# Layer 4 of a graph network on one core: four open node tiles at the start, counts widened four pieces ahead, x and own parts loaded two tiles ahead

## The chip, the cores and the metric

The kernel runs on one core of one Trainium2 chip. The metric is the time of one execution on the device in microseconds (us). The kernel before took 2745.0 us (median of 3 runs, 2740.99 to 2750.39).

## The reference

Four GraphSAGE layers over 6250 nodes and 100,000 edges sorted by target node. Layer 4 and what follows it are the part that matters here:

```python
h = jnp.maximum(_layernorm(x, axis=-1), 0.0)
...                                                   # layers 1 to 3
msum = jax.ops.segment_sum(h[src], dst, num_segments=n)
h_neigh = msum / jnp.clip(deg, 1.0)[:, None]
h = h @ W4_self + h_neigh @ W4_neigh + b4
return x + (h @ W_fc + b_fc)
```

The kernel multiplies the weights together ahead of time. So a node of layer 4 needs three things: its input row of x, an "own part" of 256 values that layer 3 left in the table `xq`, and the sum, divided by the degree, of the rows of its source nodes. Those rows stand in the table `tab_s` with 512 float32 values each (a value of 256 features, split into two addends).

## The kernel before

The 6250 nodes are 49 tiles of 128 (`NT`). Many edges end in low nodes, so layer 4 sums in two ways that run side by side.

- **Hub tiles** 0 to 21 (`H4` = 22) are dense products (`dense`, the matmul at L566). A matrix of edge counts between 128 targets and 128 sources (fp8, from `tab_a`) is multiplied with the 128x512 rows of that source tile. A hub tile takes 49 such matmuls, added up in one PSUM bank `pd`. The counts come in pieces of 5 to 7 source tiles: `load` (L1785) fetches a piece `ac` on ScalarE's DMA queue, nine pieces ahead, and `widened` (L1794) has ScalarE cast it to a 32-bit `af`. A piece is cast two pieces ahead of its products, into one of four buffers. Eight pieces make a hub tile.
- **Sum tiles** 22 to 48 go over 266 groups of 128 edges (`sums`). For each, GpSimd starts an indirect DMA (L492) that gathers 128 rows of `tab_s` into one of 14 slots of `ring`. VectorE makes a one-hot matrix `hot` (L488), TensorE multiplies (L510, into `pg`), and VectorE adds four such groups' result to the tile's `acc` (L542, L544). `hub.advance` mixes the hub matmuls in between, about four to one gather.

The source rows are kept in SBUF as eight resident tiles `zt`. Two of them, source tiles 33 to 42, are filled by layer 3. The other six are fetched from `tab_s` by SyncE (L1817) when layer 3 has ended: zt0, zt7, zt14, zt20, zt27 and zt43, named by their first source tile. Before, hub tiles 0 and 1 are opened first: their 20 products on the two kept `zt` run ahead of the gathers, then both are finished in turn, then tiles 2 to 21 follow.

When a tile is summed, `done4` calls `load4`: ScalarE's queue fetches the tile's x (`xr`, L1893) and own part (`q`, L1895), 10 buffers each. `finish4` adds the two on VectorE (L1909), adds the scaled sum (L1911), and SyncE stores the tile (L1914). For sum tiles the next tile's two loads are issued as well.

The program is written in the order of this text, but a scheduler places each engine's instructions by its own estimate of when operands and buffers come free. After that each engine runs its queue strictly in order; a DMA that has to wait holds up all that stands behind it in its queue. The plain (not gathered) DMAs of the ScalarE and SyncE queues also take turns on eight semaphores (DMAHW0 to DMAHW7). A DMA that gets a semaphore first waits until that semaphore's last user has landed, whatever queue and data that was.

Of the kernel before, what the change touches and what calls it, by code (L numbers as in the profile page):

```python
# [13 lines left out]
F32R = mybir.dt.float32r  # L14
# [7 lines left out]
P = 128  # L22
# [15 lines left out]
def _edges_below(n, E, N):  # L38

    f = math.sqrt(min(n, N) / N)  # L40
    return E * f, Z_SIGMA * math.sqrt(E * f * (1.0 - f))
# [37 lines left out]
def fast_path(  # L79
# [19 lines left out]
    FO = W_fc.shape[1]  # L99
    NT = (N + P - 1) // P  # L100
# [15 lines left out]
    for d in range(NT):  # L116
        m, s = _edges_below(d * P, E, N)
        m1, s1 = _edges_below((d + 1) * P, E, N)
# [9 lines left out]
    for d in range(NT):  # L128
        m, s = _edges_below(d * P, E, N)
        m1, s1 = _edges_below((d + 1) * P, E, N)  # L130
# [7 lines left out]
    H1, H3, H4 = HUB  # L138
# [112 lines left out]
    one_tag = {}  # L251
# [304 lines left out]
    def dense(ss, block, rows, F, psd, done, extra=0, wide=False, own=None, halved=()):  # L556

        hold = {}

        def run(s):  # L560
            if s == ss[0]:
                hold[0] = bank(psd, "pd", "pd", (2 * F if wide else F + extra,))
            a = block(s)
            z = rows(s)
            if wide:
                nc.tensor.matmul(hold[0], a, z, start=(s == ss[0]), stop=(s == ss[-1]))  # L566
            order = () if wide else (1, 0) if s in halved else (2, 0, 1)
            for part in order:
                c = extra if part == 2 else 0
                first = s == ss[0] and part == order[0]  # L570
                if s == own:
                    nc.tensor.matmul(hold[0], ident_r if s in halved else ident_b,
                                     z[:, part * F : (part + 1) * F], start=first, stop=False)
                nc.tensor.matmul(hold[0][:, : F + c], a, z[:, part * F : (part + 1) * F + c],  # L574
                                 start=(first and s != own),
                                 stop=(s == ss[-1] and part == order[-1]))
            if s == ss[-1]:
                done(hold[0])

        return [lambda s=s: run(s) for s in ss]  # L580
# [4 lines left out]
    ahead = upto2.enter_context(tc.tile_pool(name="ahead", bufs=1, side="right"))  # L585
# [77 lines left out]
    with ExitStack() as pro:  # L663
        pst = pro.enter_context(tc.tile_pool(name="pst0", bufs=3, space=PSUM))
        psm = pro.enter_context(tc.tile_pool(name="psm0", bufs=3, space=PSUM))
# [193 lines left out]
        nk = max(RB1, RB * P - RB1)  # L859
# [239 lines left out]
    with ExitStack() as on:  # L1099
        pst = on.enter_context(tc.tile_pool(name="pst1", bufs=1, space=PSUM))  # L1100
        psm = on.enter_context(tc.tile_pool(name="psm1", bufs=1, space=PSUM))
        psg = on.enter_context(tc.tile_pool(name="psg1", bufs=2, space=PSUM))
        psd = on.enter_context(tc.tile_pool(name="psd1", bufs=2, space=PSUM))
        wk = on.enter_context(tc.tile_pool(name="fl1", bufs=2))
# [30 lines left out]
        def done1(d, acc):  # L1135
# [37 lines left out]
            with behind(ended):  # L1173
                for k in range(KI):
# [11 lines left out]
                        lambda acc, d=d: todo.append(done1(d, acc)), extra=3)  # L1186
# [4 lines left out]
        hub = Hub(made.rest() + work)  # L1191
# [124 lines left out]
    with tc.tile_pool(name="fl2c", bufs=1) as ck, ExitStack() as late:  # L1316
        pst = psm = late.enter_context(tc.tile_pool(name="pst2", bufs=3, space=PSUM))
        one_tag[id(pst)] = "pw"
        psd = late.enter_context(tc.tile_pool(name="psd2", bufs=2, space=PSUM))
# [58 lines left out]
        wk = late.enter_context(tc.tile_pool(name="fl2", bufs=2))  # L1378
# [242 lines left out]
        def widened(got):  # L1621
            if 1 not in got:
                got[1] = early_pool[0].tile([P, BATCH, P], F32R, name="aw", bufs=4)
                nc.scalar.copy(got[1], got[0])  # L1624
# [36 lines left out]
        for _ in range(7):  # L1661
# [3 lines left out]
        first = [w for d in range(H1, H4)  # L1665
                 for w in build_narrow(d, (skR, mkR, RB1), npool, psb, copies)]
        hub = Hub(first, 12)
# [12 lines left out]
        for b in reversed(range(NB)):  # L1680
# [3 lines left out]
            for s0 in range(0, tb, G2):  # L1684
                X = (xmore if at // G2 % 2 else xpool).tile([P, G2, FH], F32, name="X2")
                for k in range(G2):
# [27 lines left out]
                    if at == MADE_AT:  # L1714
                        for _ in steps:
# [3 lines left out]
                                                    name="kept_rows", bufs=1))  # L1719
# [51 lines left out]

    upto2.close()

    def stream(pool, chunks, wide_pool=None, widen=lambda s: True, deep=4):

        got = {}
        where = {(d, s): i for i, (d, s0, s1) in enumerate(chunks) for s in range(s0, s1)}

        def load(i):
            if i >= len(chunks):  # L1780
                return
            d, s0, s1 = chunks[i]
            got[i] = pool.tile([P, 7, P], F8, name="ac", bufs=deep + 1)
            t = got[i][:, : s1 - s0, :]
            nc.scalar.dma_start(t.bitcast(BF16), tab_a[d, :, s0:s1, :])  # L1785

        wide = {}
        most_wide = max([s1 - s0 for _, s0, s1 in chunks if widen(s0)])

        def widened(i):  # L1790
            if i < len(chunks) and widen(chunks[i][1]):
                n = chunks[i][2] - chunks[i][1]
                wide[i] = wide_pool.tile([P, most_wide, P], F32R, name="af", bufs=4)
                nc.scalar.copy(wide[i][:, :n, :], got[i][:, :n, :])  # L1794

        for i in range(deep):
            load(i)
        if wide_pool:
            widened(0)
            widened(1)  # L1800

        def block(d, s):
            i = where[d, s]
            if s == chunks[i][1]:
                if wide_pool:
                    widened(i + 2)
                load(i + deep)
            return (wide if i in wide else got)[i][:, s - chunks[i][1], :]

        return block  # L1810
# [10 lines left out]
    with ExitStack() as on:  # L1821
        psd = on.enter_context(tc.tile_pool(name="psd3", bufs=2, space=PSUM))
        psg = on.enter_context(tc.tile_pool(name="psg3", bufs=3, space=PSUM))
        psm = on.enter_context(tc.tile_pool(name="psm3", bufs=2, space=PSUM))
        zk = on.enter_context(tc.tile_pool(name="fz4", bufs=1, side="right"))
        Z4 = {}
        z4_kept = ((33, 38), (38, 43))
        z4_late = ((0, 7), (7, 14), (14, 20), (20, 27), (27, 33), (43, NT))
# [4 lines left out]
        with tc.tile_pool(name="fl3", bufs=2) as wk:  # L1833
# [37 lines left out]
            with tc.issue_after(kept_stores[-1].ins):  # L1871
                for s0, s1 in ((EARLY[1], NT),):
                    Z3.update(resident(wk, tab_r, FH, s0, s1))
            block = stream(wk, [(d, s0, s1) for d in range(H3) for s0, s1 in late], wk,
                           lambda s: s < KEPT)
            todo = []
            work = []
            for d in range(H3):
                work += dense([s for s0, s1 in late for s in range(s0, s1)], lambda s, d=d: block(d, s), lambda s: Z3[s], FH, psd,
                              lambda acc, d=d: todo.append(done3(d, acc)), own=d,  # L1880
# [6 lines left out]
        with tc.tile_pool(name="fl4", bufs=2) as wk:  # L1887
            loaded4 = {}

            def load4(d):  # L1890
                n = P if d < NFULL else NREM
                xr = wk.tile([P, FI], F32, name="xr4", bufs=10)
                nc.scalar.dma_start(xr[:n, :], x[d * P : d * P + n, :])  # L1893
                q = wk.tile([P, FO], F32, name="q4", bufs=10)
                nc.scalar.dma_start(q[:n, :], xq[d * P : d * P + n, :])  # L1895
                loaded4[d] = n, xr, q

            def done4(d, acc):
                for i in (d, d + 1) if H4 <= d < NT - 1 else (d,):
                    if i not in loaded4:  # L1900
                        load4(i)
                return finish4(d, acc)

            def finish4(d, acc):
                n, xr, q = loaded4.pop(d)
                yield 1
                yield 1
                yield 1
                nc.vector.tensor_add(xr[:n, :], xr[:n, :], q[:n, :])  # L1909
                for c in range(0, acc.shape[1], FO):  # L1910
                    nc.vector.scalar_tensor_tensor(xr[:n, :], acc[:n, c : c + FO],  # L1911
                                                   rmean[:n, d : d + 1], xr[:n, :],
                                                   op0=ALU.mult, op1=ALU.add)
                nc.sync.dma_start(out[d * P : d * P + n, :], xr[:n, :])  # L1914

            order = [*z4_kept, *z4_late]
            block = stream(zk, [(d, *c) for d in (0, 1) for c in z4_kept]
                           + [(d, *c) for d in (0, 1) for c in z4_late]
                           + [(d, *c) for d in range(2, H4) for c in order],
                           wk, deep=9)  # L1920
            todo = []
            parts4 = []
            for d in range(H4):
                parts4.append(dense([s for s0, s1 in order for s in range(s0, s1)],
                                    lambda s, d=d: block(d, s), lambda s: Z4[s], FO, psd,
                                    lambda acc, d=d: todo.append(done4(d, acc)), wide=True))
            nk = sum(s1 - s0 for s0, s1 in z4_kept)
            hub = Hub([w for d in (0, 1) for w in parts4[d][:nk]]
                      + [w for d in (0, 1) for w in parts4[d][nk:]]
                      + [w for p in parts4[2:] for w in p])  # L1930
            hub.advance(2 * nk)
            for s0, s1 in z4_late:
                Z4.update(resident(wk, tab_s, FO, s0, s1))
            sums(wk, psg, tab_s, FO, srcE, keyE, jb, H4, done4, 14, hub, wait=4, todo=todo,
                 rest=8, wide=True)

# [642 lines left out]
```

## Time and profile before

| | |
|---|---|
| median of 3 runs | 2745.0 us |
| the profiled execution's own time | 2742.18 us |
| its span in the trace | 2740.4 us |
| granted TensorE clock, mean | 0.922 |
| first matmul of layer 4 | 2357.81 us |
| last matmul | ends 2728.45 us |
| busy shares over the span | PE 84%, DVE 76%, POOL 68%, ACT 47% |

The time outside the span is 2742.18 - 2740.4 = 1.8 us. Layer 4 is the last 383 us of the span and is the only part that the diff touches. PE is TensorE, PEld its weight loads, DVE VectorE, ACT ScalarE, POOL GpSimd, SP SyncE; a q behind the name is the engine's sequencer, which issues its DMAs. "idle before" names what an engine was waiting for when it stood still.

### The profile page before, as it was taken

To read this page: it belongs to the slowest core of one execution; us is meant where nothing else is said; L and a number is where in the kernel's file an instruction comes from. 1 tells how busy PE (TensorE), PEld (TensorE's weight loads), DVE (VectorE), ACT (ScalarE), POOL (GpSimd) and SP (SyncE) were. 2 spreads that over 40 slices of the span, in tenths; PEclk is the share of its full clock that TensorE was granted. 3 is DMA by queue.
4 is the path that set the end of the run, shared out by engine and by line. 5 is a ranking of instruction groups with operands and counts; after the bars stand their busy time and mean duration, and the time that the engine had idled before them with its cause. 6 is when DMAs were issued, how large, how long until landed. Compare 5 with 4: busy or idle time off the path is not lost.

```text
span 2740.4 us, 37738 instructions
## 1 busy us (share of the span) xinstructions
PE 2314.7 (84%) x10402; PEld 1439.0 (53%) x10402; DVE 2088.1 (76%) x5540; ACT 1299.7 (47%) x2859; POOL 1857.0 (68%) x2169
## 2 busy tenths in 40 slices
PE   4689999999786466566889999899799999789988
PEld 2356666767453232223555666655345444467776
DVE  8889777776589898898678998888376777446666
ACT  5568777764288888686423333232111111134443
POOL 5477777777566676677656676676477777657765
PEclk8799999999898588787999999999899999899999
DMA  8467777777799899899999999898899999999987
GB/s 279 152 179 209 209 208 213 217 232 221 222 356 333 299 346 336 283 336 361 328 290 301 339 349 322 275 341 292 300 376 387 381 380 351 347 323 316 319 286 226
DMA packets 365625, 809.90 MB, mean 296 GB/s; under 512 B 56238, under 2 KB 154646, under 8 KB 365372
## 3 DMA queue, kind: packets, MB, share of 16 engines
q0 software_dynamic: 143248, 501.86, 56.3%
q1 hardware_dynamic: 145928, 215.57, 21.6%
q10 hardware_dynamic: 76228, 89.96, 9.8%
q8 instruction: 85, 1.39, 0.2%
q14 instruction: 136, 1.11, 0.1%
HBM read 602.51 MB, written 205.46 MB: 295 GB/s over the span
## 4 chain that ended last, share of the span: by engine, by line
PE 48%; DMA 24%; DVE 13%; ACT 5%; issue 4%; POOL 2%; ACTq 0%; DVEq 0%; SPq 0%; POOLq 0%
PE pd L574 17%; PE pg L513 11%; DMA X<-rows,srcIf 7%; DMA xr<-in_x 4%; DVE run L1669 4%; DMA ring<-tab_h,srcT 4%; PE pm_hp L1175 3%; DMA rows<-X 3%; PE pm_prf L1558 3%; PE pm_hp L1169 2%; PE pd L566 2%; PE pb L349 2%; DVE acc L544 2%; DVE X L1669 2%; PE pm_prf L1552 2%
## 5 line engine op out<-in xcount | busy, mean ns | idle before, releaser
L1688 POOL DMA_INDIRECT X<-rows,srcIf x782 | 742.1, 949 | 368.9 <-issue 150.6
L1669 DVE SCALAR_TENSOR_TENSOR run<-run,samef,X 128x512 f32<-128x512 f32 x758 | 572.4, 755 | 49.0 <-DMA X<-rows,srcIf 43.5
L492 POOL DMA_INDIRECT ring<-tab_h,srcT x474 | 455.4, 961 | 149.9 <-issue 53.1
L513 PE MATMUL pg<-ring,hot 128*128 128x259 bf16 (+1 forms) x2292 | 475.1, 316 | 41.9 <-DMA ring<-tab_h,srcT 29.1
L544 DVE SCALAR_TENSOR_TENSOR acc<-pg,M,acc 128x256 f32<-128x256 f32 (+2 forms) x617 | 314.3, 536 | 80.9 <-PE pg L513 69.1
L492 POOL DMA_INDIRECT ring<-tab_r,srcE x290 | 293.3, 1011 | 116.2 <-issue 48.5
L1794 ACT CAST af<-ac 128x768 fp32r<-128x768 fp8e4 (+3 forms) x216 | 173.2, 805 | 398.9 <-DMA ac<-tab_a 157.8
L492 POOL DMA_INDIRECT ring<-tab_s,srcE x266 | 254.6, 957 | 124.6 <-PE pg L510 47.8
L566 PE MATMUL pd<-zt,af 128*128 128x512 f32 x1078 | 302.9, 407 | 38.1 <-ACT af L1794 31.6
L513 PEld LDWEIGHTS <-hot 128*128 128x128 bf16 x2292 | 214.3, 98 | 226.4 <-issue 103.6
L1669 DVE SCALAR_TENSOR_TENSOR X<-X,samef,run 128x512 f32<-128x512 f32 x379 | 282.1, 744 | 37.4 <-DMA X<-rows,srcIf 16.5
L574 PE MATMUL pd<-kept_rows,aw 128*128 128x512 f32 x920 | 292.2, 440 | 11.2 <-ACT aw L1624 6.3
L566 PEld LDWEIGHTS pd<-zt,af 128*128 128x128 f32 x1078 | 208.7, 196 | 95.8 <-ACT af L1794 44.6
L574 PEld LDWEIGHTS pd<-kept_rows,aw 128*128 128x128 f32 x920 | 174.7, 192 | 83.9 <-issue 35.3
L488 DVE TENSOR_SCALAR hot<-iota_bf,keyE 128x128 bf16<-128x128 bf16 (+1 forms) x556 | 142.9, 281 | 86.7 <-PE pg L513 55.3
L1558 PE MATMUL pm_prf<-unf,hTf 128*128 128x512 f32 x384 | 201.0, 647 | 1.9 <-ACT hTf L1548 1.3
L341 ACT ACTIVATE hs<-ht,onef 128x128 bf16<-128x128 bf16 x396 | 153.3, 393 | 89.4 <-PE pb L349 88.4
L1624 ACT CAST aw<-ae 128x512 fp32r<-128x512 fp8e4 x160 | 99.4, 622 | 181.3 <-PE pd L574 163.9
L574 PE MATMUL pd<-Z,A 128*128 128x256 bf16 (+1 forms) x1176 | 184.8, 274 | 0.7 <-ACT A L354 0.6
L375 ACT ACTIVATE ht<-iota_bf,skR 128x128 bf16<-128x128 bf16 x448 | 158.1, 402 | 11.0 <-DMA col<-in_L_gnn_b 8.0
L393 PE MATMUL pb<-hm,hs 128*128 128x196 bf16 x448 | 82.3, 281 | 89.8 <-ACT A L398 65.4
L340 ACT ACTIVATE ht<-iota_bf,sk 128x128 bf16<-128x128 bf16 x396 | 153.1, 398 | 8.3
(391 smaller groups left out, 4198.6 us busy)
## 6 DMA issues: line engine op xcount, KB each, us to landing
rows<-X SPq DMA_DIRECT2D x385, 256.0 KB, 4.9
tab_r<-r ACTq DMA_DIRECT2D x48, 384.0 KB, 5.9
rows<-hpf SPq DMA_DIRECT2D x49, 256.0 KB, 3.4
th<-tab_t ACTq DMA_DIRECT2D x49, 256.0 KB, 6.6
X<-rows,srcIf POOLq DMA_INDIRECT x782
tab_a<-A ACTq DMA_DIRECT2D x14, 784.0 KB, 6.0
ae<-tab_a SPq DMA_DIRECT2D x160, 64.0 KB, 5.0
tab_s<-q SPq DMA_DIRECT2D x39, 256.0 KB, 6.1
```

The source lines that it names most:

```text
L340: nc.scalar.activation(t, iota_b, AF.Abs, bias=sk[:, r : r + 1])
L341: nc.scalar.activation(hots[0], t, AF.Relu, bias=one, scale=-1.0)
L375: nc.scalar.activation(held["ht"][:, i, :], iota_b, AF.Abs, bias=sk[:, r : r + 1])
L492: nc.gpsimd.indirect_dma_start(out=ring[:, j % deep, :].bitcast(F32) if wide else ring[:, j % deep, :], out_offset=None, in_=table, in_off ...
L513: mm = nc.tensor.matmul(pg[:, : F + c], hot[j], X[:, part * F : (part + 1) * F + c], start=(k == 0 and part == 2), stop=(k == n - 1 and pa ...
L544: nc.vector.scalar_tensor_tensor(acc[d], half, m, acc[d], op0=ALU.mult, op1=ALU.add)
L566: nc.tensor.matmul(hold[0], a, z, start=(s == ss[0]), stop=(s == ss[-1]))
L574: nc.tensor.matmul(hold[0][:, : F + c], a, z[:, part * F : (part + 1) * F + c], start=(first and s != own), stop=(s == ss[-1] and part == ...
L1558: nc.tensor.matmul(pm, hT[:, c, :], un[:, c, :], start=False, stop=(c == KH - 1))
L1669: nc.vector.scalar_tensor_tensor(put, held, st, row, op0=ALU.mult, op1=ALU.max)
L1688: nc.gpsimd.indirect_dma_start(out=X[:, k, :], out_offset=None, in_=tab_p, in_offset=bass.IndirectOffsetOnAxis(ap=srcI[:, t : t + 1], axis=0),
L1794: nc.scalar.copy(wide[i][:, :n, :], got[i][:, :n, :])
```

## The change

Five edits, all in layer 4:

1. `widened` casts four pieces ahead of the products, and `af` has six buffers.
2. Hub tiles 0 to 3 are open together. Their products go piece by piece: the four tiles' first pieces, the four tiles' second pieces, and so on, through all eight. The 40 products on the two kept `zt` run ahead of the first gather's product.
3. The PSUM banks of hub tiles alternate between two pools in pairs, so that four can be open.
4. `done4` loads x and own part for the tile and the next two, for hub tiles too.
5. The stream of pieces is listed in the new order.

```diff
-    def stream(pool, chunks, wide_pool=None, widen=lambda s: True, deep=4):
+    def stream(pool, chunks, wide_pool=None, widen=lambda s: True, deep=4, ahead=2):
...
-                wide[i] = wide_pool.tile([P, most_wide, P], F32R, name="af", bufs=4)
+                wide[i] = wide_pool.tile([P, most_wide, P], F32R, name="af", bufs=ahead + 2)
...
-            widened(0)
-            widened(1)
+            for i in range(ahead):
+                widened(i)
...
-                    widened(i + 2)
+                    widened(i + ahead)
...
+        one_tag[id(psm)] = "pm"
...
-                for i in (d, d + 1) if H4 <= d < NT - 1 else (d,):
+                for i in range(d, min(d + 3, H4 if d < H4 else NT)):
...
-            block = stream(zk, [(d, *c) for d in (0, 1) for c in z4_kept]
-                           + [(d, *c) for d in (0, 1) for c in z4_late]
-                           + [(d, *c) for d in range(2, H4) for c in order],
-                           wk, deep=9)
+            first = range(4)
+            block = stream(zk, [(d, *c) for c in order for d in first]
+                           + [(d, *c) for d in range(4, H4) for c in order],
+                           wk, deep=9, ahead=4)
...
-                                    lambda s, d=d: block(d, s), lambda s: Z4[s], FO, psd,
+                                    lambda s, d=d: block(d, s), lambda s: Z4[s], FO, (psd, psm)[d // 2 % 2],
...
-            hub = Hub([w for d in (0, 1) for w in parts4[d][:nk]]
-                      + [w for d in (0, 1) for w in parts4[d][nk:]]
-                      + [w for p in parts4[2:] for w in p])
-            hub.advance(2 * nk)
+            cuts = [sum(s1 - s0 for s0, s1 in order[:i]) for i in range(len(order) + 1)]
+            hub = Hub([w for a, b in zip(cuts, cuts[1:]) for d in first for w in parts4[d][a:b]]
+                      + [w for p in parts4[4:] for w in p])
+            hub.advance(4 * nk)
```

TensorE, from the start of layer 4, before. zt_21030 and zt_21031 are the kept source rows, zt_24758, zt_24760 and zt_24762 are zt0, zt7 and zt14; `pg` are products of gathered rows:

```order
L566 MATMUL pd<-zt_21030,af 128x512 x5
L566 MATMUL pd<-zt_21031,af 128x512 x5
L510 MATMUL pg<-ring,hot 128x512 x5
L566 MATMUL pd<-zt_24758,af 128x512 x5
L510 MATMUL pg<-ring,hot 128x512
L566 MATMUL pd<-zt_24758,af 128x512 x2
L510 MATMUL pg<-ring,hot 128x512 x7
L566 MATMUL pd<-zt_24760,af 128x512 x7
L510 MATMUL pg<-ring,hot 128x512 x6
L566 MATMUL pd<-zt_24762,af 128x512 x6
```

(The first two rows stand there twice, once for each of the two tiles.) The same place in the changed program, where zt_24800 is zt0:

```order
L566 MATMUL pd<-zt_21030,af 128x512 x20
L566 MATMUL pd<-zt_21031,af 128x512 x20
L510 MATMUL pg<-ring,hot 128x512 x5
L566 MATMUL pd<-zt_24800,af 128x512 x5
L510 MATMUL pg<-ring,hot 128x512
L566 MATMUL pd<-zt_24800,af 128x512 x4
L510 MATMUL pg<-ring,hot 128x512
L566 MATMUL pd<-zt_24800,af 128x512 x4
```

Twice as many products run ahead of the first gather's product, and each late `zt` now serves 24 or 28 products, with one gather's product after every four or so, before the next `zt` is needed. Before, it served 6 or 7.

SyncE's queue, the loads of the late `zt` before, with the semaphores that each waits for:

```order
L1817 DMA zt7_24760<-tab_s_68 128x7x512
L1817 DMA zt14_24762<-tab_s_68 128x6x512 [waits DMAHW2_49]
L1817 DMA zt20_24764<-tab_s_68 128x7x512 [waits DMAHW3_49]
L1817 DMA zt27_24766<-tab_s_68 128x6x512 [waits DMAHW5_49]
L1817 DMA zt43_24768<-tab_s_68 128x6x512 [waits DMAHW4_49]
```

and in the changed program:

```order
L1817 DMA zt7_24802<-tab_s_68 128x7x512
L1817 DMA zt14_24804<-tab_s_68 128x6x512 [waits DMAHW6_49]
L1817 DMA zt20_24806<-tab_s_68 128x7x512 [waits DMAHW3_49]
L1817 DMA zt27_24808<-tab_s_68 128x6x512 [waits DMAHW3_49]
L1817 DMA zt43_24810<-tab_s_68 128x6x512 [waits DMAHW2_49]
```

The four last waits moved to other semaphores. By the values waited for, zt14 now waits for zt0 to land, zt20 for a piece of counts, zt27 for zt20, and zt43 for a piece of counts. Before, zt14, zt20, zt27 and zt43 waited for pieces of counts and own parts on ScalarE's queue.

ScalarE's queue in the changed program, at the casts of the four pieces for zt20 (af_25002 is the first tile's, the two casts above it are the last for zt14):

```order
L1794 CAST af_24962<-ac_24867 128x768 [waits PE_49]
L1896 DMA q4_25127<-xq_70 128x256 [waits DMAHW6_49]
L1785 DMA ac_25059<-tab_a_69 128x384 [waits DMAHW7_49,Activation_49]
L1894 DMA xr4_25129<-in_x 128x256 [waits DMAHW0_49]
L1794 CAST af_24977<-ac_24886 128x768 [waits PE_49]
L1896 DMA q4_25131<-xq_70 128x256 [waits DMAHW1_49]
L1785 DMA ac_25073<-tab_a_69 128x384 [waits DMAHW3_49,Activation_49]
L1794 CAST af_25002<-ac_24908 128x896 [waits PE_49]
```

Here the load of ac_25073 has the semaphore DMAHW3 after zt27, so it waits for zt27 to land, and the casts for zt20 stand behind it. In the same way the first cast for zt27 stands behind a load that waits for zt43. Before, the loads that wait for zt0, zt7, zt14 and zt20 stood on this queue, with eight loads of x and seven of own parts among them. In the changed program the first load of x stands behind the cast of the second piece for zt14.

## The prediction

> **What bounds the kernel now.** The diff touches layer 4 alone, so the table by stages comes first. Its columns are the stage, its length, the busy time of PE, PEld, DVE, ACT and POOL with instruction counts, the granted clock, the DMA engines' busy share and GB/s.
>
> ```profile
> 2357.80:2420.00 62.20, 41.37 (x98) 27.95 (x99) 19.01 (x62) 11.53 (x14) 38.83 (x41) 0.68 1.02 391
> 2420.00:2442.00 22.00, 22.00 (x98) 18.07 (x97) 11.57 (x34) 11.79 (x14) 8.88 (x10) 1.00 0.81 248
> 2442.00:2452.00 10.00, 10.00 (x46) 8.26 (x45) 7.28 (x23) 4.07 (x5) 7.56 (x9) 1.00 0.96 323
> 2452.00:2697.00 245.00, 227.43 (x964) 179.86 (x963) 155.79 (x485) 106.00 (x125) 179.12 (x187) 0.99 0.93 306
> 2697.00:2728.50 31.50, 31.50 (x140) 25.90 (x139) 21.85 (x68) 14.30 (x17) 20.24 (x21) 1.00 0.80 251
> ```
>
> PE's counts are matmuls of 512 columns, so they measure progress: 1344 are to be done (1078 hub, 266 gathered). Unhindered, one takes 31.5/140 = 0.225 us. In the first 62 us, the ramp, only 98 are done, the work of 22 us: 40 us are lost there. In the 245 us after 2452 one takes 0.254 us, and 28 us are lost. These are the two places where the change can win.
>
> The ramp waits for the late `zt`. The chain of waits has this in it (start, us, what):
>
> ```profile
> 2357.48 23.77 DMA zt<-tab_s
> 2381.33 0.33 ACTq L1785
> ```
>
> zt7 lands at 2381.25. A load of counts waited for that semaphore on ScalarE's queue, and the casts waited behind it. The timeline shows the next `zt` in the same way:
>
> ```profile
> 2357.81 7.58 PE L566 MATMUL pd<-zt,af 128*128 128x512 f32 x20 [5.64 <-ACT af L1794]
> 2371.12 2.34 PE L566 MATMUL pd<-zt,af 128*128 128x512 f32 x5
> 2392.64 2.90 PE L566 MATMUL pd<-zt,af 128*128 128x512 f32 x6 [4.99 <-DMA zt<-tab_s]
> 2406.30 0.33 ACTq L1785 DMA_DIRECT2D ac<-tab_a  x1
> 2406.70 0.36 SPq L1817 DMA_DIRECT2D zt<-tab_s  x1
> 2418.99 4.62 PE L566 MATMUL pd<-zt,af 128*128 128x512 f32 x19 [2.35 <-ACT af L1794]
> ```
>
> zt0 is there by 2371.1, zt14 at 2392.6, and the count load at 2406.3 is the one that waits for zt20. zt27 is issued only then.
>
> In the long stage the lines and the waits agree on something that the busy shares hide:
>
> ```profile
> L1909 DVE TENSOR_TENSOR xr<-xr,q 128x256 f32<-128x256 f32 x34 | 14.5, 426 | 88.3 <-DMA xr<-in_x 86.6 <-DMA out<-xr 1.7
> L492 POOL DMA_INDIRECT ring<-tab_s,srcE x187 | 179.2, 958 | 66.1 <-issue 22.2 <-PE pg L510 22.0 <-PE pd L566 21.9
> PE pd L566 <- ACT af L1794: 16.8, 16, 2.6
> ```
>
> VectorE works 155.8 us and stands 88.3 us in front of the x that `finish4` adds. That is 244.1 of 245 us: VectorE, 64% busy, is what sets the pace. The chain goes round: x lands, VectorE goes on and ends another tile, its store lands, the buffer takes the next x.
>
> ```profile
> 2670.08 4.09 DMA xr<-in_x
> 2674.26 0.42 DVE xr L1909
> 2678.28 4.36 DMA out<-xr
> 2682.74 4.11 DMA xr<-in_x
> ```
>
> GpSimd is close behind. A gather takes 0.958 us and 0.30 us pass before the next is issued (22.2 us in 73 cases), so 1.258 us at least: 187 of them are 235 of the 245 us. Its last gather, and TensorE's end after it, stand here:
>
> ```profile
> 2722.65 0.95 POOL L492 DMA_INDIRECT ring<-tab_s,srcE  x1 [0.31 <-PE pg L510]
> 2727.98 0.47 PE pg L510 x2
> ```
>
> So TensorE ends at 2728.45, 5.8 us after the last gather's issue. The rest to 2740.4 is VectorE's last sums and the stores, which the change leaves as they are.
>
> **The change part by part.** No matmul, gather or byte is added or removed. Everything is order.
>
> *Four open tiles, in the ramp.* Start and casts of the kept pieces are as before. 40 products now run ahead: the first 20 at the row's 7.58 us (the clock is low after the pause), the others at 4.62/19 = 0.243: done at 2357.8 + 7.6 + 4.9 = 2370.3. zt0 is there at 2371; five gathered products fill the gap. Then come 34 matmuls of zt0 with its gathers (7.7 us, to about 2380), zt7 at 2381.3, 35 matmuls to about 2390, zt14 at 2392.6. I take these landings as they were, since the same gathers run beside them and 19 loads of counts replace the mixture of counts, x and own parts. After zt14, two DMA issues and a cast (0.33 + 0.33 + 0.94) start its 30 matmuls at 2394.4; a cold start makes them 7.6 + 10 x 0.225 = 9.8 us, to 2404.
>
> Here the order shows a new wait. The load of ac_25073 waits for zt27, and the casts for zt20 stand behind it. zt27 waits for zt20 to land, at 2406. So TensorE stands still from 2404 until zt27 lands. Who waits: TensorE, and with it the ring, which is full with 24 + 14 = 38 gathers issued by about 2405 (2357.8 + 38 x 1.258 = 2405.6). What zt27 costs has no row of its own kind. Sharing the engines, zt20 took 2406.3 - 2392.6 = 13.7 us. Alone, zt27 and zt43 together (2 x 1.57 MB) need 8 us at the 391 GB/s of the first stage, zt27 half of that. I take 9 us, the middle, since gathers in flight still share the engines when it begins but no new ones come: zt27 at 2415, zt43 at about 2419, products again at 2416.5 after a cast. The remaining 95 matmuls of the four tiles take 7.6 + 75 x 0.225 = 24.5 us: four hub tiles and 43 gathered products, 239 matmuls, stand at 2441. Before, at 2441, 98 + 21 x 98/22 = 191.5 were done. That is 47.5 ahead, 10.7 us.
>
> The extra stop also cools TensorE. By the rows a start after a pause costs 7.58 - 20 x 0.225 = 3.1 us. The Trainium skill ("TensorE: Matmul & The Clock Gate", Part 1, on the HAM clock gate) speaks against such stops: an idle window of about 3.4 us halves the clock, and about 3.4 us of work bring it back. By that a cold start would lose 1.7 us, and the sum would come out 1.4 us lower for each; the row is longer and is used.
>
> *Four-ahead casts, six buffers.* The casts are the same in number. In the long stage TensorE waited 16.8 us for casts, 2.6 us at most at a time; a piece lasts 245 us/125 casts = 1.96 us, so two more pieces cover each single stop. But VectorE's round sets the pace there, and the casts only follow. I put nothing for it by itself; if VectorE's waits were gone, it would be worth those 16.8 us.
>
> *Two tiles ahead.* The loads of x cannot run further ahead than 10 buffers, before or after. What moves is when the ten fill up. Before, ten pairs of x and own part go out in the ramp (2.6 MB of its 24.3 MB), and from then on each x waits for a store. The scheduler places the add 15 matmuls behind the load of x on average for the 34 loads of the long stage (3.8 us at 0.254), less than the loop's 4.1 us landing and its issue, and VectorE waits 86.6/34 = 2.55 us per add. After, 39 loads come behind matmul 235. The first ten have the add 27 matmuls behind (6.1 us at 0.225); the other 29 again 15. So ten adds wait about 2.55 + 3.8 - 6.1 = 0.3 us, 3 us in all, and 29 wait 74 us. VectorE from matmul 239 to the last x (966 matmuls, as the 964 before): 966/964 x 155.8 + 74 + 3 = 233 us, to 2674, and 31.5 us without x loads behind it: 2705.5. If the first ten wait as long as the others, 22 us more: 2728.
>
> *GpSimd's floor.* 38 gathers by 2405, the others from about 2416.5 on: the last is issued at 2416.5 + 227 x 1.258 = 2702, and TensorE ends 5.8 us later, at 2708.
>
> *Sum.* The end is between 2708 and 2728. I take 2713: near the floor, because the planned distance of the ten adds nearly doubles, with 5 us (my choice) because stops of VectorE and GpSimd do not always fall together. The last matmul moves from 2728.45 to 2713, by 15.4 us. The profiled execution took 2742.18 us, so 2726.8; the runs' median lies 2.8 us above it: about 2730. PSUM banks in two pools cost nothing: each is free four tiles earlier.
>
> **The rivals.**
>
> *A, more is won.* Casts far ahead free TensorE, the ring never stays full, GpSimd sets the pace from the start. Its last gather is at 2357.8 + 265 x 1.258 = 2691, TensorE's end 2697: 31.5 us, 2711 for the profiled run, 2713 to 2722 for the median with small losses. For it: GpSimd already fills 235 of 245 us. Against: the queue behind zt27. Chance 0.15.
>
> *B, the DMA engines are the bound.* The ramp has them full:
>
> ```profile
> DMA packets 12816, 24.34 MB, mean 391 GB/s; under 512 B 1248, under 2 KB 5472, under 8 KB 12814
> ```
>
> The five stages' busy shares times their lengths add to 344 us. If layer 4 cannot do better than the long stage's 0.93, that is 370 us, and it takes 370.7 now: no change, 2744. The Trainium skill ("Trainium Kernel Development and Optimization", Key Constraints) says that the DMAs of the SyncE, ScalarE and GpSimd queues run on the same 16 engines and interleave. By that an earlier issue of one only takes from another; the 1.02 of the first stage agrees. Against it: that same 1.02 is 9% above 0.93. Chance 0.15.
>
> *C, the new queue stop is dearer.* zt27 takes zt20's 13.7 us and zt43 another 10.2 (zt7's pace, 2381.3 - 2371.1). Then the 60 matmuls of zt27 and zt43 start at 2431.7 and end at about 2448, 3.4 us ahead of before. With the 3 to 5 us of the ten adds, 2736 to 2740: the same. Chance 0.08.
>
> *D, slower.* VectorE has no slack in the long stage, so any longer wait per x goes straight into the end. ScalarE's queue has four-piece-ahead casts ahead of an x load, and stores share the engines with everything else. If the 39 adds wait one us more each, 39 us come on: 2742.2 - 15.4 + 39 + 2.8 = 2769. It decides from (15.4 + 8.2)/39 = 0.6 us more per add. For it: waits go up to 6.1 us now. Against: the planned distances are no shorter than before. Chance 0.12.
>
> **How the numbers follow.** The forecast (2722 to 2737) has 0.50. A difference under 0.3% (8.2 us) can't be told from none here. Faster: forecast and A, 0.65. Same: B and C, 0.23. Slower: D, 0.12. The range goes from 2716 (most of A) to 2749 (B with the spread of the runs, and the beginning of D); D's larger part and A's lower end, some 0.15, are left out.
>
> **What would show it.** Right: after the start 40 hub products in a row; TensorE idle for about 10 us near 2405 and then products on zt20 behind the landing of zt27; 239 matmuls by about 2441; the first ten waits at the add of x (L1910 then) short, the later ones 2 to 3 us; VectorE's work plus waits again filling the stage to the last x; a last gather near 2705. Wrong: zt20's products before zt27 lands; under 200 matmuls at 2441 (B or C); VectorE's waits over 110 us in the long stage (D); a GpSimd that never waits for TensorE after 2420 (A).

## The result and the profile after

The changed kernel takes 2728.99 us (median of 20 runs, 2724.11 to 2733.88), the kernel before 2741.32 beside it. The ratio is 0.9956, 95% interval 0.9947 to 0.9965: 12.3 us faster, where 2730 was forecast. In the profiled execution (2732.06 us, span 2730.3) layer 4 begins 3.0 us later than in the one of before, so from here on times are counted from layer 4's first hub product: 2360.84 us after, 2357.81 before.

First the stages, each cut at the same distance from that product, of the kernel before (columns as in the prediction's table; PE's count in brackets is the matmuls done):

```profile
2357.80:2441.00 83.20, 62.37 (x190) 45.23 (x191) 29.58 (x93) 22.74 (x28) 47.01 (x50) 0.76 0.97 356
2441.00:2527.00 86.00, 81.64 (x350) 64.70 (x348) 54.75 (x170) 36.51 (x44) 64.13 (x68) 1.00 0.96 317
2527.00:2667.00 140.00, 128.46 (x543) 102.16 (x544) 90.56 (x283) 62.15 (x74) 101.14 (x106) 0.99 0.93 303
2667.00:2684.00 17.00, 15.63 (x67) 11.90 (x65) 8.78 (x29) 6.05 (x7) 12.34 (x14) 1.00 0.93 289
```

and of the changed kernel:

```profile
2360.80:2444.00 83.20, 65.09 (x246) 51.12 (x247) 30.29 (x97) 30.75 (x37) 52.95 (x56) 0.85 1.01 371
2444.00:2530.00 86.00, 84.97 (x372) 69.39 (x371) 61.07 (x191) 37.09 (x45) 65.29 (x69) 1.00 1.00 348
2530.00:2670.00 140.00, 128.06 (x537) 100.44 (x537) 88.96 (x277) 59.01 (x71) 106.48 (x111) 0.99 0.94 308
2670.00:2687.00 17.00, 13.88 (x53) 10.53 (x52) 9.78 (x31) 9.04 (x11) 10.65 (x12) 0.90 0.85 263
...
2444.00:2687.00 243.00, 226.91 (x960) 180.36 (x960) 159.80 (x499) 105.15 (x125) 182.41 (x190) 0.99 0.95 319
```

The balance can be read off in matmuls. After the first 83.2 us the changed kernel is 56 ahead, at 0.225 us each 12.6 us: the ramp alone is as large as the whole gain. The next 86 us add 22 (TensorE at 86/372 = 0.231 us per matmul, before 86/350 = 0.246). The 140 us after that take 6 back, and the next 17 us 14 (67 were done there before), most of it in one pause of TensorE without a releaser, 2.61 us, which a second profile of the same kernel doesn't have (62 matmuls there):

```profile
2676.20 0.60 PE L510 MATMUL pg<-ring,hot 128*128 128x512 f32 x1 [2.61 <-issue]
```

The ramp, in TensorE's timeline; every stop there of over 1 us is here (idle before and its releaser in brackets):

```profile
2360.84 11.80 PE L566 MATMUL pd<-zt,af 128*128 128x512 f32 x40 [5.63 <-ACT af L1794]
2384.69 0.47 PE L566 MATMUL pd<-zt,af 128*128 128x512 f32 x1 [2.96 <-DMA zt<-tab_s]
2396.57 1.22 PE L566 MATMUL pd<-zt,af 128*128 128x512 f32 x2 [3.68 <-ACT af L1794]
2406.28 1.73 PE L566 MATMUL pd<-zt,af 128*128 128x512 f32 x4 [2.63 <-ACT af L1794]
2418.09 1.22 PE L566 MATMUL pd<-zt,af 128*128 128x512 f32 x2 [8.80 <-ACT af L1794]
```

The last stop is the new wait that the prediction named: TensorE has 120 hub products done (40 and those of zt0, zt7 and zt14) and stands before the first product on zt20. The chain of waits follows it back from zt20's landing to zt27's, to a load of counts on ScalarE's queue and the cast behind it:

```profile
2375.13 33.04 DMA zt<-tab_s
2408.19 8.46 DMA zt<-tab_s
2416.73 0.33 ACTq L1785
2417.10 0.94 ACT af L1794
```

The long stage, by lines, from 2444 to 2687 (count, busy time and mean ns of one, idle before it and its releasers):

```profile
L1910 DVE TENSOR_TENSOR xr<-xr,q 128x256 f32<-128x256 f32 x38 | 16.1, 424 | 79.5 <-DMA xr<-in_x 56.6 <-issue 9.3 <-DMA q<-xq 8.8
L492 POOL DMA_INDIRECT ring<-tab_s,srcE x190 | 183.1, 964 | 60.7 <-issue 21.0 <-PE pg L510 17.1 <-PE pd L566 14.0
L566 PE MATMUL pd<-zt,af 128*128 128x512 f32 x771 | 212.0, 396 | 9.8 <-ACT af L1794 9.8
```

VectorE works 159.8 us (the last of the windows above) and stands 79.5 in front of the add of x, together 239 of 243 us; before it was 244 of 245. But GpSimd is full as well: 111 gathers in the 140 us are 1.261 us each, and 1.258 is the least that it needs. Which of two engines that both fill the stage sets the pace can't be told from their rows, and that is what the experiments are about. The end:

```profile
2712.28 0.95 POOL L492 DMA_INDIRECT ring<-tab_s,srcE  x1 [0.30 <-PE pd L566]
2717.58 1.97 PE L510 MATMUL pg<-ring,hot 128*128 128x512 f32 x8
```

Layer 4's last group of eight gathered products starts 356.7 us after its first hub product; before it was 370.0 (2727.82 less 2357.81).

### The profile page after: what moved, and what is told of

The parts are those of the page before. It is cut to its first block, busy times and chain, and to the rows that moved or that the text cites. A ratio compares the mean times of both kernels' runs of the same rounds, so it can differ in the third digit from the quotient of the medians.

```text
span 2730.3 us, 37722 instructions
## 1 busy us (share of the span) xinstructions
PE 2303.3 (84%) x10402; PEld 1436.1 (53%) x10402; DVE 2084.6 (76%) x5540; ACT 1301.6 (48%) x2859; POOL 1858.7 (68%) x2169
## 3 DMA queue, kind: packets, MB, share of 16 engines
q0 software_dynamic: 143248, 501.86, 56.3%
## 4 chain that ended last, share of the span: by engine, by line
PE 49%; DMA 26%; DVE 13%; issue 5%; ACT 2%; POOL 2%; ACTq 0%; DVEq 0%; POOLq 0%; SPq 0%
PE pd L574 18%; PE pg L513 11%; DMA X<-rows,srcIf 9%; DMA ring<-tab_h,srcT 4%; DVE run L1669 3%; PE pm_hp L1175 3%; PE pm_prf L1558 3%; DMA rows<-X 2%; DMA xr<-in_x 2%; PE pm_hp L1169 2%; PE pb L349 2%; DVE acc L544 2%; DVE X L1669 2%; DMA out<-xr 2%; PE pm_prf L1552 2%
## 5 line engine op out<-in xcount | busy, mean ns | idle before, releaser
L513 PE MATMUL pg<-ring,hot 128*128 128x259 bf16 (+1 forms) x2292 | 475.1, 316 | 45.9 <-DMA ring<-tab_h,srcT 34.8
L544 DVE SCALAR_TENSOR_TENSOR acc<-pg,M,acc 128x256 f32<-128x256 f32 (+2 forms) x617 | 314.6, 536 | 79.5 <-PE pg L513 71.1
L492 POOL DMA_INDIRECT ring<-tab_s,srcE x266 | 255.4, 960 | 110.5 <-PE pg L510 34.8
```

The costliest lines, as they stand in the source:

```text
L492: nc.gpsimd.indirect_dma_start(out=ring[:, j % deep, :].bitcast(F32) if wide else ring[:, j % deep, :], out_offset=None, in_=table, in_off ...
L513: mm = nc.tensor.matmul(pg[:, : F + c], hot[j], X[:, part * F : (part + 1) * F + c], start=(k == 0 and part == 2), stop=(k == n - 1 and pa ...
L544: nc.vector.scalar_tensor_tensor(acc[d], half, m, acc[d], op0=ALU.mult, op1=ALU.add)
```

## The experiments

The theory to be tried: the four open tiles carry the gain, casts and loads carry nothing, and what the long stage could have given ended at GpSimd's floor. The rivals: the casts carry it; the loads carry it; VectorE's waits for x set the pace; the bytes on the DMA engines do. All results in one table: median and ratio to the kernel before, run beside it, and from each profile the matmuls done in the first 83.2 us, the next 86 and the next 140, and where the last gather and TensorE's last group start, in us from the first hub product.

| kernel | median us | ratio (95%) | matmuls | last gather | last group |
|---|---|---|---|---|---|
| before | 2741 to 2743 | 1 | 190, 350, 543 | 364.8 | 370.0 |
| changed, first set | 2728.99 | 0.9956 (0.9947 to 0.9965) | 246, 372, 537 | 351.4 | 356.7 |
| changed, again | 2730.64 | 0.9959 (0.9943 to 0.9976) | 250, 375, 541 | 348.9 | 352.9 |
| four open tiles only | 2736.16 | 0.9976 (0.9961 to 0.9991) | 244, 336, 528 | 360.2 | 363.5 |
| casts four ahead only | 2740.83 | 0.9989 (0.9976 to 1.0002) | 190, 375, 529 | 363.8 | 369.2 |
| loads two ahead only | 2742.49 | 0.9991 (0.9975 to 1.0006) | 180, 360, 532 | 367.5 | 370.6 |
| changed, old loads | 2727.80 | 0.9939 (0.9920 to 0.9959) | 247, 371, 544 | 348.5 | 353.8 |
| changed, 20 x buffers | 2720.22 | 0.9927 (0.9904 to 0.9949) | 249, 379, 572 | 348.1 | 351.6 |
| changed, 27 plain loads | 2730.76 | 0.9961 (0.9944 to 0.9978) | 241, 367, 517 | 357.5 | 364.1 |
| old loads, ring of 19 | 2731.18 | 0.9959 (0.9944 to 0.9975) | 232, 376, 526 | 350.3 | 361.9 |

(With 20 buffers the last group is of two.) The two profiles of the changed kernel differ by 3.8 us in the last column: that much a single profile can't tell. A profile shows one execution, and not always a middling one: that of the changed kernel's second set is the shortest of ten (2715.62), that of the plain loads the longest of eleven (2739.97). So kernels are ranked by the medians, and the three columns show where the matmuls are won.

### One part at a time

*Four open tiles only*: the changed kernel with

```
-                           wk, deep=9, ahead=4)
+                           wk, deep=9, ahead=2)
-                for i in range(d, min(d + 3, H4 if d < H4 else NT)):
+                for i in (d, d + 1) if H4 <= d < NT - 1 else (d,):
```

> Only the four open tiles; casts two pieces ahead in four buffers and loads of x as before the change. Theory 1 (the ramp carries the gain, and the two other parts are worth nothing): 10 to 13 us under the kernel before (ratio 0.995 to 0.996), some 240 matmuls done 83 us after layer 4's first matmul, against 191 before. Rival 1 (the casts four ahead carry it): at most 3 us, ratio 0.999 to 1.000. Rival 2 (x two tiles ahead carries it): the same as rival 1.

Measured: 6.9 us under the kernel before, between the theory's 10 and the rivals' 3. The windows show how:

```profile
2358.20:2441.40 83.20, 64.71 (x244) 51.39 (x245) 32.25 (x105) 28.16 (x34) 52.66 (x55) 0.86 1.02 374
2441.40:2527.40 86.00, 78.50 (x336) 62.06 (x335) 57.87 (x180) 36.11 (x43) 64.69 (x69) 1.00 0.98 332
```

The ramp gives all it gives in the changed kernel, 244 matmuls, without the casts. But the next 86 us do 336 where the changed kernel does 372. TensorE's timeline has seven stops there, 7.5 us in all, each of them a wait for a cast; the first three:

```profile
2461.79 1.20 PE L566 MATMUL pd<-zt,af 128*128 128x512 f32 x4 [0.60 <-ACT af L1794]
2474.34 0.73 PE L566 MATMUL pd<-zt,af 128*128 128x512 f32 x2 [2.43 <-ACT af L1794]
2482.95 1.20 PE L566 MATMUL pd<-zt,af 128*128 128x512 f32 x4 [0.62 <-ACT af L1794]
```

*Casts only*: the kernel before with `bufs=ahead + 2`, `widened(i + ahead)` and `ahead=4`.

> Only the casts four pieces ahead in six buffers. Theory 1: within 2 us of the kernel before (ratio 0.999 to 1.001), although TensorE's 16.8 us of waits for casts in the long stage shrink. Rival 1: 8 to 12 us faster, ratio 0.996 to 0.997.

Measured: 2.2 us, and the interval reaches over 1. The theory holds for the part alone, at the edge of its 2 us. Its profile does 375 matmuls in the 86 us after the ramp against 350, and only 529 against 543 in the 140 us behind them: of the 25 that the casts win, 14 are given back.

*Loads only*: the kernel before with

```
-                for i in (d, d + 1) if H4 <= d < NT - 1 else (d,):
+                for i in range(d, min(d + 3, H4 if d < H4 else NT)):
```

> Only x and own parts two tiles ahead. Theory 1: within 2 us of the kernel before (ratio 0.999 to 1.001), since the ten buffers hold the loads back. Rival 2: 8 to 12 us faster, ratio 0.996 to 0.997.

Measured: 0.6 us, nothing that can be told. VectorE waits for x as long as before (243 us from 2439.4 on, by lines; 83.3 us in 33 adds before):

```profile
L1909 DVE TENSOR_TENSOR xr<-xr,q 128x256 f32<-128x256 f32 x34 | 14.5, 426 | 81.2 <-DMA xr<-in_x 80.2 <-DMA out<-xr 1.1
```

*Old loads*: the changed kernel with that line put back.

> The changed kernel with the loads of x put back to where they were. Theory 1: as the changed kernel within 2 us (ratio 0.995 to 0.996 of before). Rival 2: the gain falls to under 3 us (ratio 0.999 to 1.000). Rival 1: as theory 1.

Measured: 15.3 us under the kernel before, in six runs; its interval overlaps that of the changed kernel. So the loads bring nothing here either. Without the loads, tiles and casts together gain 15.3 us in the medians (16.2 in the layer's length, 370.0 less 353.8), and apart 6.9 and 2.2 (6.5 and 0.8). The casts are worth nearly nothing alone and some 8 us behind the new ramp: these are the stops in front of casts, which the old loads with four-ahead casts don't have:

```profile
2440.00:2526.00 86.00, 84.73 (x371) 69.17 (x369) 61.73 (x194) 37.23 (x45) 65.59 (x68) 1.00 1.00 346
```

### What holds the long stage

In the first set of these every run, those of the kernel before too (median 3154.04), took over 3090 us, with pauses for which the trace names no releaser. Its ratios are compared only among themselves, and two of its kernels were run again in a set without such pauses, the quiet set. The changed kernel itself was not run in the set with pauses; the nearest to it there is the one with 20 x buffers, 0.9967.

*Without some gathers* (in the set of 3150 us), and *plain loads* (in both sets). The first leaves out every eighth gather after the first 48, the second loads as many bytes of other rows from SyncE. The edit of the second:

```
-                gather(j)
+                if wide and j % 8 == 7 and j - j0 >= 48:
+                    nc.sync.dma_start(ring[:, j % deep, :].bitcast(F32), table[j % 48 * P : (j % 48 + 1) * P, :])
+                else:
+                    gather(j)
```

> The changed kernel without every eighth gather of layer 4 after the first 48 (some 27 of 266; the products use what lies in the ring slot). Theory 1 (GpSimd's floor): 27 x 1.26 = 34 us less of GpSimd, the long stage falls towards TensorE's 0.231 us per matmul as in its first 86 us, 10 to 20 us under the changed kernel (0.988 to 0.992 of before). Rival 3 (VectorE's waits for x): within 3 us of the changed kernel (0.995 to 0.997). Rival 4 (the bytes on the DMA engines): 27 x 0.26 MB = 7.1 MB less at 319 GB/s, some 20 us, 0.988.

> The changed kernel with the same 27 gathers replaced by plain loads of 128 rows of the same table, issued by SyncE (other rows, as many bytes). Theory 1: GpSimd is relieved as without them: 10 to 20 us under the changed kernel (0.988 to 0.992 of before). Rival 4 (the bytes): no gain, within 3 us of the changed kernel (0.995 to 0.997). Rival 3: within 3 us as well, or slower, since the stores of SyncE's queue stand behind loads that wait for a ring slot.

> The changed kernel with 27 of the 266 gathers replaced by plain loads of as many bytes from SyncE, now where few pauses without a releaser are in the way. Theory 1 (GpSimd's 1.26 us per gather is the floor of the long stage): 8 to 20 us under the changed kernel, 2709 to 2721 (0.988 to 0.993 of before). Rival 3 (VectorE's waits for x) and rival 4 (the bytes): within 3 us of the changed kernel, 2726 to 2732.

Measured in the set with pauses: 0.9836 (0.9789 to 0.9884) without the gathers, 0.9875 (0.9831 to 0.9920) with plain loads. There GpSimd stands 59.7 us without a releaser between its gathers in layer 4 (the changed kernel with 20 x buffers, same set; the row is in the last section), and both kernels that relieve it are well under the one with 20 x buffers. In the quiet set the same plain loads give 0.9961, the changed kernel's time (0.9959). GpSimd, relieved of 27 gathers, only waits longer for ring slots that TensorE hasn't read (243 us from 2444.76 on):

```profile
L492 POOL DMA_INDIRECT ring<-tab_s,srcE x164 | 157.6, 961 | 87.4 <-PE pg L513 43.4 <-PE pd L569 23.6 <-issue 18.3
L1913 DVE TENSOR_TENSOR xr<-xr,q 128x256 f32<-128x256 f32 x38 | 16.2, 427 | 84.4 <-DMA xr<-in_x 74.8 <-DMA q<-xq 9.5
```

So GpSimd's floor does not by itself bound the changed kernel, and my theory of the long stage falls as it was put. The plain loads alone would fit a bound by bytes as well; the next kernel, which moves as many bytes and is faster, speaks against that. One reserve: SyncE's stores stood behind the plain loads, and VectorE waited 84.4 us for x, 5 to 9 more than in the changed kernel's two profiles (79.5 and 75.7). That could hide a gain of as many us, but not the upper part of the 8 to 20 expected.

*Twenty buffers for x* (in both sets):

```
-                xr = wk.tile([P, FI], F32, name="xr4", bufs=10)
+                xr = wk.tile([P, FI], F32, name="xr4", bufs=20)
```

> The changed kernel with twenty buffers for x in place of ten, so that a load of x no longer waits for a store of ten tiles before. Theory 1 (GpSimd's 1.26 us per gather sets the pace of the long stage, VectorE's waits for x lie beside it): VectorE's waits for x fall from 79.5 us to under 40 in the 243 us, and the time is at most 6 us under the changed kernel, 2723 to 2729 (ratio to before 0.993 to 0.996). Rival 3 (VectorE's waits for x set the pace, as the prediction had it): 10 to 20 us under it, 2709 to 2719 (0.988 to 0.992).

> The changed kernel with twenty buffers for x. Theory 1: VectorE's waits for x fall to under 40 us, the time by at most 6 us, 2723 to 2729. Rival 3: 10 to 20 us under the changed kernel, 2709 to 2719.

Measured: 0.9967 (0.9936 to 0.9999) in the set with pauses. In the quiet set 2720.22 us, 10.4 under the changed kernel beside it (the two intervals, 0.9904 to 0.9949 and 0.9943 to 0.9976, just overlap); the fastest kernel of all, 21 us under the one before. VectorE's waits at the add are more than halved (32.5 us for the 38 adds that waited 79.5; 37.7 with the last tile's 5.2), TensorE no longer waits for a cast at all, and it runs at 0.227 us per matmul in the 86 us (243 us from 2436.64 on, by lines):

```profile
L1910 DVE TENSOR_TENSOR xr<-xr,q 128x256 f32<-128x256 f32 x38 | 16.1, 423 | 32.5 <-DMA q<-xq 21.8 <-DMA xr<-in_x 10.5
L566 PE MATMUL pd<-zt,af 128*128 128x512 f32 x819 | 219.8, 391 | 0.0
L492 POOL DMA_INDIRECT ring<-tab_s,srcE x192 | 185.3, 965 | 58.7 <-PE pd L566 18.9 <-PE pg L510 17.2 <-issue 14.0
```

and by windows:

```profile
2436.64:2522.64 86.00, 86.00 (x379) 70.82 (x379) 70.34 (x220) 41.62 (x50) 65.13 (x68) 1.00 1.02 361
2522.64:2662.64 140.00, 135.78 (x572) 104.89 (x571) 95.04 (x289) 63.46 (x75) 106.43 (x111) 1.00 0.95 312
```

That the waits for casts go too fits the order of ScalarE's queue, where the loads of x stand between the casts: a load that waits for a store holds up every cast behind it. In front of casts ScalarE waits 13.5 us for stores in the changed kernel's 243 us, and 2.8 here. And now the end looks different. TensorE has its hub products done and waits for each gathered tile:

```profile
2701.55 0.95 POOL L492 DMA_INDIRECT ring<-tab_s,srcE  x1 [0.30 <-issue]
2703.52 0.77 PE L510 MATMUL pg<-ring,hot 128*128 128x512 f32 x1 [0.96 <-DMA ring<-tab_s,srcE]
2705.00 1.57 PE L510 MATMUL pg<-ring,hot 128*128 128x512 f32 x2 [0.72 <-DMA ring<-tab_s,srcE]
```

The number of gathers per stage is that of the changed kernel (68 and 111 against 69 and 111), and so is the last one's place, 348.1 us against 348.9 and 351.4. So GpSimd's floor is the next bound, a few us below the changed kernel. VectorE's waits and this floor seem to lie so close together that relieving GpSimd alone wins nothing, and that halving VectorE's waits wins a few us and then meets the floor. A kernel that relieves both was not run. How many us the waits cost is not settled: the medians say 10.4 (2720.22 us is between the ranges of the two theories), and the layer's own length says 1.3 to 5.1 (351.6 against 352.9 and 356.7).

### What holds the ramp

*zt27 and zt43 issued on GpSimd's queue, ahead of the gathers* (in the set of 3150 us):

```
-        nc.sync.dma_start(zt.bitcast(F32) if two else zt,
+        (nc.gpsimd if two and s0 in (27, 43) else nc.sync).dma_start(zt.bitcast(F32) if two else zt,
```

> The changed kernel with the loads of zt27 and zt43 issued on GpSimd's queue ahead of layer 4's gathers, so that nothing waits for zt20 to land before they go out. Theory 1 (the 8.8 us stop of TensorE is the wait of zt27 for zt20 and of the count load for zt27): the stop shrinks to under 3 us and the time is 3 to 8 us under the changed kernel (0.993 to 0.995 of before). Rival 4 (the DMA engines are full in the ramp, 1.02 of 16, so bytes only change places): the earlier zt and the gathers land later by as much, TensorE stands elsewhere, within 3 us of the changed kernel (0.995 to 0.997).

Measured: 0.9974 (0.9945 to 1.0003), no better than 20 buffers in the same set, so no gain from it is shown. The long stop before zt20's products is gone. Others are there instead, the gathers' behind the two loads and TensorE's in front of the first gathered product, and 239 matmuls are done in 83.2 us (264 with 20 buffers in that set):

```profile
2737.50 0.94 POOL L492 DMA_INDIRECT ring<-tab_s,srcE  x1 [3.96 <-DMA zt<-tab_s]
2745.17 0.77 PE L510 MATMUL pg<-ring,hot 128*128 128x512 f32 x1 [8.44 <-DMA ring<-tab_s,srcE]
```

*A ring of 19* (in the quiet set), the changed kernel with the old loads and

```
-            sums(wk, psg, tab_s, FO, srcE, keyE, jb, H4, done4, 14, hub, wait=4, todo=todo,
+            sums(wk, psg, tab_s, FO, srcE, keyE, jb, H4, done4, 19, hub, wait=4, todo=todo,
```

> The changed kernel with the loads of x where they were, and a ring of 19 gathered tiles in place of 14. Theory 1: GpSimd stands still in the ramp for some 14 us with the ring full; five slots more take 5 x 1.26 = 6 us of that stop, every later gather and the end come 4 to 6 us earlier than with the old loads alone (2727.8): 2720 to 2724, 0.991 to 0.993 of before. Rival 3: within 2 us of the old loads alone. Rival 4 (bytes): the five gathers (1.3 MB, 3.4 us at 390 GB/s) delay zt27 by as much, and the end comes no earlier.

Measured: 2731.18, no gain over the old loads alone (2727.80 in its own set). The bytes rival is right for the ramp. The five gathers do go out early, and zt27 lands later: the load of counts that waits for it goes out 59.9 us after the first hub product, with the old loads alone 56.3, and 3.4 us were expected for the bytes. TensorE's stop there is 11.0 us, with the old loads alone 9.1, and only 232 matmuls are done in 83.2 us, 15 fewer. The load of counts with the old loads (first product at 2356.82) and with the ring of 19 (2357.23), and the ring's stop and ramp:

```profile
2413.07 0.33 ACTq L1785 DMA_DIRECT2D ac<-tab_a  x1
...
2417.16 0.33 ACTq L1785 DMA_DIRECT2D ac<-tab_a  x1
2418.52 1.22 PE L566 MATMUL pd<-zt,af 128*128 128x512 f32 x2 [10.96 <-ACT af L1794]
2357.23:2440.43 83.20, 62.12 (x232) 48.73 (x233) 25.51 (x83) 28.82 (x35) 55.23 (x58) 0.83 1.00 371
```

*The changed kernel again*, as the base of that set:

> The changed kernel itself, so that the other runs of this set stand beside it on one chip. Every theory: 0.995 to 0.996 of the kernel before where the engines issue without pauses as in the first traces; with the pauses without a releaser that the last set showed on all engines, nearer to 1 (0.997).

Measured: 0.9959 (0.9943 to 0.9976), as the first time.

## Why the prediction was right, and where not

**The ramp: right, nearly to the row.** 40 products run ahead, in 11.8 us where 12.5 were worked out. zt7's products start 23.9 us after the start (23.5 forecast), zt14's at 35.7 (36.6). The new wait of a count load for zt27 is there: zt27 lands at 55.8 (57.2), and TensorE's stop before the products on zt20 is 8.8 us where 12.5 were forecast, since a stop of 2.6 us on a cast came before it. 246 matmuls stand at 83.2 us where 239 were forecast; 56 ahead where 47.5 were.

**A cold start** was put at 3.1 us. The 40 products at 0.225 would be 9.0, so it cost 2.8 here. By an estimate from the Trainium skill ("TensorE: Matmul & The Clock Gate", Part 1) it would be 1.7 us; this trace shows more. Over the first products of ten profiles it goes from 1.8 (20 in 6.28 us, casts only) to 3.4 (40 in 12.38, the changed kernel again), so a single row can't price it.

**The casts: the step that failed.** "I put nothing for it by itself" is right for the part alone, 0.9989. But the forecast's ramp kept its 47 matmuls to the end with nothing said of the casts, and the run of the four tiles alone loses some 8 us again to stops in front of casts. The prediction's reason was that VectorE's round sets the pace, so that casts are worth something only where VectorE's waits are gone. They are not gone: in the 86 us behind the ramp VectorE stands 27.9 us in front of the add with the four tiles alone and 24.2 in the changed kernel, and fills the stage with work and waits both times. Yet the changed kernel does 36 matmuls more there (372 and 336). First the four tiles alone, then the changed kernel, for these 86 us:

```profile
L1910 DVE TENSOR_TENSOR xr<-xr,q 128x256 f32<-128x256 f32 x14 | 5.9, 424 | 27.9 <-DMA xr<-in_x 18.2 <-issue 7.1 <-DMA ac<-tab_a 2.6
...
L1910 DVE TENSOR_TENSOR xr<-xr,q 128x256 f32<-128x256 f32 x16 | 6.8, 423 | 24.2 <-DMA q<-xq 8.8 <-issue 5.8 <-DMA xr<-in_x 4.9
```

The sum came out all the same, since both parts are in the change.

**Two tiles ahead: the waits nearly right, their cause not.** The prediction had the first ten adds wait 0.3 us and the other 29 2.55, 3 and 74 us in all. Measured were 9.4 us for the first ten behind the ramp and 76.3 for the others. But this is not the loads' doing: with the old loads it is 9.3 and 73.7, alone the move is worth 0.6 us, and the changed kernel is no slower without it. The first ten wait 25.1 us before the change, 18.4 with the four tiles alone, 14.6 with the casts alone: it takes both. The forecast put its sum near the floor because of these ten adds, so that it came out is luck in this part.

**VectorE sets the pace: right in sign, far too strong.** Halving its waits took 47 us of waiting off VectorE (79.5 to 32.5 in 38 adds) and 1 to 10 us off the time. A wait that fills an engine's stage to the last us is not for that reason the stage's bound; GpSimd was as full, and relieving it alone brought nothing.

**GpSimd's floor.** It was put at 2702 us, 344.2 from the start. Measured were 351.4 and 348.9, and 348.1 with VectorE's waits halved: the ramp's stop of 10 us was in the forecast, some pauses and longer gathers were not.

**The rivals.** A (more is won) did not come about: GpSimd stood still behind the full ring for 10.4 us in the ramp, as argued against it. B (the DMA engines bind, no change) fell as to the time: they were taken to give no more than 0.93 in the long stage, and in the 86 us after the ramp they gave 1.00 at 348 GB/s. For the ramp alone it holds, as the ring of 19 shows; the Trainium skill's rule that the DMAs of the SyncE, ScalarE and GpSimd queues run on the same 16 engines ("Trainium Kernel Development and Optimization", Key Constraints) agrees with those 15 matmuls. C had zt27 land at 62.2 us (2406.3 and 13.7); it landed at 55.8. D (longer waits at the adds) did not happen: 2.09 us per add (79.5/38), 2.55 before.

The layer was forecast to be 15.4 us shorter at TensorE's end and is 13.3 us shorter, or 17.1 in the second profile.

## What to carry to other kernels

While a ramp is held up by loads that fill the DMA engines, win by doing more work per loaded byte (each late `zt` serves four open tiles in a row here, before the change one); reordering those loads, or letting gathers run ahead of them, only moved the stop in the two runs that tried it. An edit that is worth nothing alone can be what keeps another edit's gain: try the parts apart and together before dropping one. When two engines each fill a stage with work and waits, no row says which one binds; relieve each by itself, look at what the other then does, and relieve both.

## What the runs showed of the hardware

In one set every kernel took some 15% longer, with no change in the program, at a mean granted clock of 0.888 (20 x buffers) where the profile before has 0.922. It was not the chip as such: the quiet set was taken after it on the same one. The gathers themselves took as long as ever (965 ns and 0.30 us to the next), but idle time without a releaser came in between on all engines: over the whole kernel 300 us of TensorE's (5 in the changed kernel's first profile), 256 of ScalarE's (8) and 128 of VectorE's (17). In layer 4's gathers, with 20 x buffers, it is 59.7 us (the ordinary 0.30 between two gathers partly among them), where in the changed kernel's first profile no releaser has over 34.8 us:

```profile
L492 POOL DMA_INDIRECT ring<-tab_s,srcE x266 | 256.7, 965 | 149.0 <-issue 59.7 <-PE pg L510 40.7 <-PE pd L566 23.6
2851.44 0.94 POOL L492 DMA_INDIRECT ring<-tab_s,srcE  x1 [2.12 <-issue]
```

The changed kernel:

```profile
L492 POOL DMA_INDIRECT ring<-tab_s,srcE x266 | 255.4, 960 | 110.5 <-PE pg L510 34.8
```

What causes them stays open. With them the plain loads are 0.9875 of the kernel before, against 0.9961 without, where they gain nothing over the changed kernel. A verdict on a bound holds only for the conditions in which it was measured.
